# Score packs, value products and probability transfers regrouped over the two slots of a pair

## The chip, the cores and the metric

The kernel runs on one core of one Trainium2 chip. The metric is device time in microseconds (us) from start to end of one execution; lower is better. Engines in this document: PE (TensorE, matmul), PEld (its weight loads), DVE (VectorE), ACT (ScalarE), POOL (GpSimd), SP (SyncE, which here only issues transfers). Everything is float32.

## The reference, cut to what matters

Two layers run on x of shape (16, 256, 256). Layer 0 is a diagonal complex recurrence gated by a two-matrix MLP; the change leaves it alone. Layer 1 is causal attention with 16 heads over 256 positions, with compressed keys and values, gated by a mixture of LoRA experts:

```python
x = x + s * g                                   # layer 0
xn = _layernorm(x, axis=-1)
q = (x @ Wq).reshape(B, S, N_HEADS, QK_DIM)     # nope and rope parts
c_kv = c_kv * rsqrt(mean(c_kv * c_kv) + eps) * kv_norm_w
kv = (c_kv @ Wkv_b).reshape(B, S, N_HEADS, QK_NOPE + V_DIM)
scores = where(mask, einsum('bqhd,bkhd->bhqk', q, k) * scale, min)
attn = softmax(scores, axis=-1)
out = einsum('bhqk,bkhd->bqhd', attn, v).reshape(B, S, N_HEADS * V_DIM) @ Wo
g = silu(base(xn) + 2 * lora(xn))               # top 2 of 8 experts
x = x + out * g
```

The kernel folds the key and value expansions into the query and output weights, so keys and values have 64 latent columns (and 64 rope columns for the keys) that all heads share.

## The kernel before, in words

**Chunks, groups, units, slots.** The 4096 tokens are 8 chunks of 512 tokens, two batch rows each. Layer 0 runs chunk by chunk and fills about the first 266 us. Then a written-out loop (lines 1653 to 1745) runs over 64 units. Unit i belongs to chunk ch = i // 8; r = i % 8 is its place in the chunk. Its head group is n = i // 2 (four heads), its batch row is b = i % 2. One pass of the loop is called slot i here. Even slots have b = 0, odd slots b = 1; a pair of slots is one head group.

**The order is hand-written.** PE, DVE, ACT, POOL and SP are each wrapped in `InOrder` (lines 45 to 65), which chains every instruction to the one before it on that engine. So each engine runs its instructions in the order in which the loop writes them, and a wait holds up everything behind it on that engine. All these instructions are recorded with the wrapper's line, L53; the profile's groups are told apart by their tile names.

**One unit.** The 128 partitions hold 4 heads x 32 queries, and the 256 queries are 8 blocks a = 0..7; block a needs 32(a+1) keys.

- `score_pack(u, pi)`, lines 1369 to 1403: pack 0 is blocks 7 and 6, pack 1 is blocks 5, 4, 3, pack 2 (the short one) blocks 2, 1, 0. PE writes the pack's scores into one PSUM bank (tile `sc`, a pool of 3 banks); DVE adds the causal mask on the diagonals (`sc<-sc,kmask`) and takes negated row maxima (`nm<-sc`); ACT does the exponentials into `pr` with their sums in `sr` (`pr<-sc,nm`). Short packs of even units from i = 6 on are done as two halves of 64 weight columns (128*64 in the profile).
- `normalise(u, packs)`, line 1405: DVE takes reciprocals of `sr`, POOL multiplies `pr` by them (`pr<-pr,sr`).
- `turn(u, z)`, line 1418, z = 0, 1, 2: DVE transposes 32x32 blocks of `pr` into `turned`; z = 0 needs blocks 0 to 3, z = 1 and 2 need blocks 4 to 7.
- `send(u)`, line 1430: four DMAs from SP, 192 KB each, from `turned` to a DRAM tile `far`.
- `fetch(n, y, b)`, line 1444: one DMA from SP, 384 KB, reads half y of batch row b back into `pT`, of which there are 3 buffers. It waits until the sends of that row have landed.
- `values_of(n)`, line 1490: PE multiplies both rows of group n by the values, 16 products in float32 (32 records, four 64x64 tiles of the array at once), into two banks `av`; ACT copies them to `attT`.
- `turn_here`, line 1456: for the last two units PE transposes instead.

**Queries.** Group n is made ahead: `query_mm(n, t)` for t = 0..3 (two 512-column products each, tile `pq`), `query_mul` on DVE for t = 0, 1 (`qmul<-pq,rot_q`), `query_lat` on ACT for t = 2, 3 (`qg<-pq`), `query_rot` on POOL (`qrot`), and `query_move(n)`, eight 64 KB DMAs from SP.

**What else stands in the slots**, and the change leaves in its place: r = 0 `mid_chunk` (PE transposes `pmT`, ACT copies to `mT`), `gate_begin` (PE `pg`, whose third and sixth products read `mT`; DVE `h`, ACT tanh) and `norm_begin` (DVE statistics); r = 1 `gate_end` and `gate_begin`; r = 2 `gate_end`, `norm_end` (four DVE instructions `xn<-x,mv,rs`, behind pack 0's maxima), and at the slot's end `transpose_chunk` (PE `tp<-ident,xn`); r = 4 `kv_begin`; r = 5 `kv_end`; r = 6 `router_chunk` (PE `pm`, then some 20 small DVE instructions from `lg` to `mid`); r = 7 `key_chunk` (PE `pk`, ACT `kT`); and at r = 3, 4, 5, 7 `fast_end` (PE `po`, the output projection of the chunk before), with `fast_begin` on POOL at r = 4 to 7 and 0. PSUM tiles other than `sc` share 5 banks (pool `m1`).

**The slot before**, as PE runs it: even: pack 0, `pq` 3, pack 1, `values_of` for group (i-4)/2, pack 2, then what r adds; odd: pack 0, `pq` 0, pack 1, `pq` 1, pack 2, `pq` 2, then what r adds. Unit i's turns 1, 2, 0 and its send stand in slot i+1. Group n's fetches stand in slots 2n+2 (row 0) and 2n+3 (row 1), its products in slot 2n+4; `values_of(0)` is an exception and stands in slot 5.

Of the kernel before, what the change touches and what calls it, by code (L numbers as in the profile page):

```python
# [11 lines left out]
F32 = mybir.dt.float32  # L12
# [6 lines left out]
P = 128  # L19
B, S, D = 16, 256, 256  # L20
NTOK = B * S
CH = 512
# [19 lines left out]
def tile_two_layers(ctx: ExitStack, tc: tile.TileContext, d: dict, out: bass.AP):  # L42
# [384 lines left out]
        gp.tensor_tensor(q.rot[:, 0, :], m0[:, 0, :], m1_[:, 1, :], ALU.subtract)  # L427
        gp.tensor_tensor(q.rot[:, 1, :], m1_[:, 0, :], m0[:, 1, :], ALU.add)

    def query_move(n):  # L430
        q = groups[n]
        for r in range(2):
            for h in range(G):
                sp.dma_start(
                    q.qg[64 + 32 * r : 96 + 32 * r, :, h, :],
                    q.rot[32 * h : 32 * h + 32, r, :].rearrange("p (a q) -> p a q", q=32),
                )
# [921 lines left out]
    class Unit:  # L1359


        def __init__(self, i):
            self.i = i
            self.ch, r = divmod(i, 2 * NG)
            self.g, self.b = divmod(r, 2)
            self.n = f"{self.ch}_{self.g}_{self.b}"
            self.pr = prs[i % NPR]

    def score_pack(u, pi):
        k, b, pack = chunks[u.ch], u.b, PACK[pi]  # L1370
        if pi == 0:
            u.nm = sm1.tile([P, NQ], F32, tag="nm", name=f"nm_{u.n}", bufs=3)
            u.sr = sm1.tile([P, NQ], F32, tag="sr", name=f"sr_{u.n}", bufs=3)
        qg = groups[u.i // 2].qg
        sc = ps_sc.tile([P, CH], F32, tag="sc", name=f"sc_{u.n}_{pi}")
        halves = 2 if pi == 2 and u.b == 0 and u.i > 4 else 1
        m = P // halves
        for a, o in pack:
            w = qg[:, b * NQ + a, :, :].rearrange("p h q -> p (h q)")
            for y in range(halves):  # L1380
                pe.matmul(
                    sc[m * y : m * y + m, o : o + 32 * (a + 1)], w[:, m * y : m * y + m],
                    k.kT[:, b * S : b * S + 32 * (a + 1)], start=True, stop=True,
                )
        ends = [o + 32 * (a + 1) for a, o in pack]
        step = ends[1] - ends[0]
        n = len(pack)
        assert ends == [ends[0] + step * z for z in range(n)]
        if ends[0] - 32 + step * n <= CH:
            diag = sc[:, ends[0] - 32 : ends[0] - 32 + step * n].rearrange("p (n s) -> p n s", n=n)[:, :, 0:32]  # L1390
        else:
            diag = sc[:, ends[0] - step : ends[-1]].rearrange("p (n s) -> p n s", n=n)[:, :, step - 32 : step]
        ve.tensor_tensor(diag, diag, bc(kmask, n), ALU.add)
        for a, o in pack:
            ve.tensor_reduce(
                u.nm[:, a : a + 1], sc[:, o : o + 32 * (a + 1)], AX.X, ALU.max, negate=True
            )
        for a, o in pack:
            w = 32 * (a + 1)
            ac.activation(  # L1400
                u.pr[:, OFF[a] : OFF[a] + w], sc[:, o : o + w], AF.Exp,
                bias=u.nm[:, a : a + 1], accum_out=u.sr[:, a : a + 1],
            )

    def normalise(u, packs):
        blocks = [a for pi in packs for a, _ in PACK[pi]]
# [37 lines left out]
    def fetch(n, y, b):  # L1444

        q = groups[n]
        if y == b == 0:
            q.pT = {}
        if b == 0:
            q.pT[y] = pp.tile([P, G, 3 * P], F32, tag="pT", name=f"pT_{n}_{y}", bufs=3)  # L1450
        sp.dma_start(
            q.pT[y][64 * b : 64 * b + 64].rearrange("p h q -> p (h q)"),
            q.far[b].rearrange("(y k) s h z q -> y (k s) (h z q)", y=2)[y],
        )
# [198 lines left out]
    for i in range(LAST):  # L1653
        ch, r = divmod(i, PER)
        odd = i % 2 == 1
        u, w = units[i], units[i - 1] if i else None
        here = w is not None and w.i >= LAST - 2
        n = (i + 3) // 2 if odd else (i + 2) // 2
        n = n if n < len(groups) else None
        more = ch + 1 < NCH  # L1660
        last = ch - 1 if ch == NCH - 1 and r in FINISH else None
        fast = ch - 1 if 0 < ch < NCH - 1 else None

        if not odd and n is not None:
            query_move(n)
        if odd and i > 2:
            fetch((i - 3) // 2, 0, 1)
            fetch((i - 3) // 2, 1, 1)
        elif i and not odd:
            fetch((i - 2) // 2, 0, 0)  # L1670
        score_pack(u, 0)
        if w:
            normalise(w, (2,))
        if fast is not None and r > 3:
            fast_begin(fast, r)
        if ch > 1 and r == 0:
            fast_begin(ch - 2, 0)
        out_weights(i)
        if r == 1:
            gate_end(ch, 0)  # L1680
        if r == 2:
            gate_end(ch, 1)
            if more and ch:
                norm_end(ch + 1)
        if r == 5 and more:
            kv_end(ch + 1)
        if i == LAST - 1:

            finish_mm(last, 3, 0, NPAIR)
            finish_out(last, 3)  # L1690
            last = None
        if w:
            for z in (1, 2):
                turn_here(w, z) if here else turn(w, z)

        if r == 0:
            mid_chunk(ch)
        if r == 7 and more:
            key_chunk(ch + 1)
        if n is not None:  # L1700
            query_mm(n, 0 if odd else 3)
            if not odd:
                query_lat(n, 3)
        if i == 5:
            values_of(0)
        score_pack(u, 1)

        if odd and n is not None:
            query_mm(n, 1)
            query_mul(n, 0)  # L1710
        if w:
            if here:
                turn_here(w, 0)
            else:
                turn(w, 0)
                send(w)
        if not odd:
            if i > 4:
                values_of((i - 4) // 2)
            if i:  # L1720
                fetch((i - 2) // 2, 1, 0)
        score_pack(u, 2)
        normalise(u, (0, 1))

        if odd and n is not None:
            query_mm(n, 2)
            query_mul(n, 1)
            query_rot(n)
            query_lat(n, 2)
        if r < 2:  # L1730
            gate_begin(ch, r)
        if r == 0 and more and ch:
            norm_begin(ch + 1)
        if r == 2 and more:
            transpose_chunk(ch + 1)
        if r == 4 and more:
            kv_begin(ch + 1)
        if r == 6 and more:
            router_chunk(ch + 1)
        if last is not None:  # L1740
            j = FINISH.index(r)
            finish_mm(last, j, 0, NPAIR)
            finish_out(last, j)
        if fast is not None and r in FINISH:
            fast_end(fast, r)
# [1 line left out]

    ch = NCH - 1
    u0, u1 = units[LAST - 2], units[LAST - 1]
    normalise(u1, (2,))  # L1750

    finish_mm(ch, 0, 0, 4)
    finish_mm(ch, 1, 0, 4)
    values_of(LAST // 2 - 2)
# [85 lines left out]
```

## Time and profile before

| | us |
|---|---|
| median of 3 runs | 905.29 (903.8 to 905.55) |
| the profiled execution, its own time | 903.67 |
| its span, first to last instruction | 901.9 |
| PE busy / PEld busy | 889.3 / 666.8 |
| DVE busy | 667.4 |
| POOL busy | 571.2 |
| ACT busy | 476.0 |

The profile is of one execution. Its span is 1.8 us shorter than that execution's own time. "Busy" is the union of an engine's recorded instructions; PE's ends are modelled, so the start of the next record tells more than the end of one. Records of float32 products come in pairs (x2 in counts). In a timeline row, the columns are start, length, engine, line, operation, tiles, shape and count; a bracket gives idle time ahead of the row and what ended it. "PEclk" is the granted share of the TensorE clock. Matmul weights are given as 128*128, 128*64 or 64*64 (rows*columns of the array).

From DMA issue to landing the profile gives 4.4 us (median) for a `far<-turned` piece, 4.9 us for `pT<-far` and 2.7 us for `qg<-qrot`.

### The profile page before, as it was taken

To read this page: it belongs to the slowest core of one execution; us is meant where nothing else is said; L and a number is where in the kernel's file an instruction comes from. 1 tells how busy PE (TensorE), PEld (TensorE's weight loads), DVE (VectorE), ACT (ScalarE), POOL (GpSimd) and SP (SyncE) were. 2 spreads that over 40 slices of the span, in tenths; PEclk is the share of its full clock that TensorE was granted. 3 is DMA by queue.
4 is the path that set the end of the run, shared out by engine and by line. 5 is a ranking of instruction groups with operands and counts; after the bars stand their busy time and mean duration, and the time that the engine had idled before them with its cause. 6 is when DMAs were issued, how large, how long until landed. Compare 5 with 4: busy or idle time off the path is not lost.

```text
span 901.9 us, 17976 instructions
## 1 busy us (share of the span) xinstructions
PE 889.3 (99%) x5688; PEld 666.8 (74%) x5688; DVE 667.4 (74%) x2017; ACT 476.0 (53%) x1562; POOL 571.2 (63%) x885
## 2 busy tenths in 40 slices
PE   9999999999999989999999999999999999999988
PEld 8777999987757657776776777677677767766766
DVE  6886678764687869678868867886886788687642
ACT  3234665644436646655655565565556556556441
POOL 2229687787355537787586677758667775876531
PEclk9999999999999999999999999999999999999989
DMA  9730000000024888887887887788788768878880
GB/s 276 245 118 1 1 2 1 1 1 1 1 32 79 230 209 198 186 207 161 217 218 169 206 181 201 180 217 214 170 200 211 190 170 209 210 176 194 209 223 29
DMA packets 197406, 134.04 MB, mean 149 GB/s; under 512 B 143104, under 2 KB 187968, under 8 KB 197312
## 3 DMA queue, kind: packets, MB, share of 16 engines
q1 hardware_dynamic: 195184, 128.69, 58.0%
q0 software_dynamic: 1152, 3.67, 1.2%
q8 instruction: 46, 0.75, 0.4%
q10 hardware_dynamic: 976, 0.53, 0.2%
q14 instruction: 48, 0.39, 0.1%
HBM read 63.11 MB, written 52.95 MB: 129 GB/s over the span
## 4 chain that ended last, share of the span: by engine, by line
PE 93%; DVE 3%; DMA 2%; POOL 1%; ACT 1%; SPq 0%; issue 0%; ACTq 0%; POOLq 0%
PE pq L53 23%; PE sc L53 14%; PE po L53 11%; PE av L53 8%; PE f L53 7%; PE r L53 7%; PE pg L53 5%; PE ph L53 5%; PE pf L53 5%; PE pm L53 2%; PE pkv L53 2%; PE tp L53 2%; DMA far<-turned 1%; DMA pT<-far 1%; PE pb L53 1%; PE py L53 1%
## 5 line engine op out<-in xcount | busy, mean ns | idle before, releaser
L53 POOL TENSOR_SCALAR pr<-pr,sr 128x256 f32<-128x256 f32 (+7 forms) x512 | 192.5, 397 | 188.2 <-DVE sr L53 180.3
L53 ACT ACTIVATE pr<-sc,nm 128x256 f32<-128x256 f32 (+7 forms) x512 | 190.2, 382 | 217.1 <-DVE sr L53 139.6
L53 PEld LDWEIGHTS sc<-kT,qg 128*128 128x128 f32 (+1 forms) x1198 | 150.8, 176 | 54.8 <-issue 41.6
L53 PE MATMUL sc<-kT,qg 128*128 128x32 f32 (+6 forms) x1198 | 169.0, 290 | 0.0
L53 DVE TENSOR_REDUCE nm<-sc 128x1 f32<-128x256 f32 (+7 forms) x512 | 127.5, 301 | 6.6
L53 DVE STREAM_TRANSPOSE turned<-pr 128x512 f32<-128x512 f32 x186 | 123.2, 687 | 11.0 <-POOL pr L53 10.9
L53 PE MATMUL pq<-xnT,wlat 128*128 128x512 f32 x256 | 122.7, 602 | 0.0
L53 PE MATMUL pq<-xnT,wrope 128*128 128x512 f32 x256 | 120.2, 593 | 0.0
L53 ACT ACTIVATION_READ_ACCUMULATOR pr<-sc,nm 128x1 f32 x512 | 104.0, 203 | 0.0
L53 PE MATMUL av<-pT,rowv 64*64 64x512 f32 (+2 forms) x992 | 80.5, 445 | 6.0 <-DMA pT<-far 6.0
L53 POOL TENSOR_TENSOR qrot<-qmul,qmul 128x512 f32<-128x512 f32 x64 | 83.6, 1329 | 2.8 <-DVE qmul L53 2.8
L53 DVE TENSOR_TENSOR sc<-sc,kmask 128x96 f32<-128x96 f32 (+1 forms) x192 | 45.2, 236 | 53.8 <-PE sc L53 52.5
L53 DVE TENSOR_TENSOR qmul<-pq,rot_q 128x512 f32<-128x512 f32 x128 | 80.7, 672 | 0.1
L53 ACT ACTIVATE qg<-pq 64x512 f32<-64x512 f32 x128 | 75.5, 590 | 4.3 <-PE pq L53 3.5
L53 PEld LDWEIGHTS av<-pT,rowv 64*64 64x64 f32 x992 | 39.8, 135 | 43.6 <-issue 30.1
L53 PEld LDWEIGHTS pq<-xnT,wrope 128*128 128x128 f32 x256 | 45.7, 191 | 32.4 <-issue 32.1
L53 PEld LDWEIGHTS pq<-xnT,wlat 128*128 128x128 f32 x256 | 45.7, 191 | 31.6 <-issue 31.6
L53 PEld LDWEIGHTS po<-wout,attT 128*128 128x128 f32 x416 | 59.3, 193 | 9.8 <-issue 3.5
L53 PE MATMUL po<-wout,attT 128*128 128x128 f32 (+1 forms) x416 | 65.3, 311 | 0.0
L53 POOL TENSOR_TENSOR attT<-attT,attT 128x512 f32<-128x512 f32 x36 | 45.1, 1273 | 0.0
L53 POOL TENSOR_TENSOR rs<-ve,mhalf 128x4 f32<-128x4 f32 (+1 forms) x17 | 16.8, 987 | 41.1 <-DVE ve L53 33.6
L53 PE MATMUL pf<-p2T,hT 128*128 128x256 f32 x192 | 42.7, 380 | 0.0
(229 smaller groups left out, 1520.0 us busy)
## 6 DMA issues: line engine op xcount, KB each, us to landing
far<-turned SPq DMA_DIRECT2D x248, 192.0 KB, 4.4
pT<-far SPq DMA_DIRECT2D x124, 384.0 KB, 4.9
qg<-qrot SPq DMA_DIRECT2D x256, 64.0 KB, 2.7
x<-in_x_dram SPq DMA_DIRECT2D x7, 512.0 KB, 10.4
out_dram<-x POOLq DMA_DIRECT2D x12, 256.0 KB, 4.0
wqn_wo<-in_wq_nopeT_dram SPq DMA_DIRECT2D x4, 512.0 KB, 5.4
wqn_wo<-in_Wo_dram SPq DMA_DIRECT2D x4, 512.0 KB, 6.8
p2T<-in_proj2T_dram SPq DMA_DIRECT2D x2, 512.0 KB, 8.3
```

The source lines that it names most:

```text
L53: r = getattr(self.engine, name)(*args, **kw)
```

## The change

1. `score_pack` is split into `score_mm` (PE) and `score_exp` (mask, maxima, exponentials). Packs 0 and 1 go through the same steps as before.
2. The short packs of both units of a pair are done together, in the odd slot, by the new `score_small(w, u)`: both packs' products into one bank (the odd unit's at column 256), then `score_exp` of the even unit and `score_exp` of the odd unit. All short packs are now done in halves of 64 weight columns.
3. `values_of` moves from the even slots to the odd slots, directly ahead of `score_small`; group n's products stand in slot 2n+5 (group 0's already stood in slot 5).
4. The normalisations of blocks 2, 1, 0 of both units stand in the odd slot, behind `query_mul(n, 0)`.
5. Turn 0 and send of the even unit move to the next even slot, so that both sends of a pair stand there, with `query_move` between them (before, `query_move` stood first).
6. All four fetches of group n stand in slot 2n+3: row 0 and row 1 of half 0 at its start, half 1 behind `values_of`.
7. At the end, turn 0 of unit 62 (by PE) stands behind the last slot. `query_move` gets a parameter that no call uses.

```diff
@@ -1365,23 +1365,25 @@
             self.g, self.b = divmod(r, 2)
             self.n = f"{self.ch}_{self.g}_{self.b}"
             self.pr = prs[i % NPR]
-
-    def score_pack(u, pi):
-        k, b, pack = chunks[u.ch], u.b, PACK[pi]
-        if pi == 0:
+            self.nm = None
+
+    def score_mm(u, pi, sc, base=0):
+        k, b = chunks[u.ch], u.b
+        qg = groups[u.i // 2].qg
+        m = P // 2 if pi == 2 else P
+        for a, o in PACK[pi]:
+            w = qg[:, b * NQ + a, :, :].rearrange("p h q -> p (h q)")
+            for y in range(0, P, m):
+                pe.matmul(
+                    sc[y : y + m, base + o : base + o + 32 * (a + 1)], w[:, y : y + m],
+                    k.kT[:, b * S : b * S + 32 * (a + 1)], start=True, stop=True,
+                )
+
+    def score_exp(u, pi, sc, base=0):
+        if u.nm is None:
             u.nm = sm1.tile([P, NQ], F32, tag="nm", name=f"nm_{u.n}", bufs=3)
             u.sr = sm1.tile([P, NQ], F32, tag="sr", name=f"sr_{u.n}", bufs=3)
-        qg = groups[u.i // 2].qg
-        sc = ps_sc.tile([P, CH], F32, tag="sc", name=f"sc_{u.n}_{pi}")
-        halves = 2 if pi == 2 and u.b == 0 and u.i > 4 else 1
-        m = P // halves
-        for a, o in pack:
-            w = qg[:, b * NQ + a, :, :].rearrange("p h q -> p (h q)")
-            for y in range(halves):
-                pe.matmul(
-                    sc[m * y : m * y + m, o : o + 32 * (a + 1)], w[:, m * y : m * y + m],
-                    k.kT[:, b * S : b * S + 32 * (a + 1)], start=True, stop=True,
-                )
+        pack = [(a, base + o) for a, o in PACK[pi]]
         ends = [o + 32 * (a + 1) for a, o in pack]
         step = ends[1] - ends[0]
         n = len(pack)
@@ -1401,6 +1403,19 @@
                 u.pr[:, OFF[a] : OFF[a] + w], sc[:, o : o + w], AF.Exp,
                 bias=u.nm[:, a : a + 1], accum_out=u.sr[:, a : a + 1],
             )
+
+    def score_pack(u, pi):
+        sc = ps_sc.tile([P, CH], F32, tag="sc", name=f"sc_{u.n}_{pi}")
+        score_mm(u, pi, sc)
+        score_exp(u, pi, sc)
+
+    def score_small(u, v):
+
+        sc = ps_sc.tile([P, CH], F32, tag="sc", name=f"sc_{u.n}_2")
+        for z, y in enumerate((u, v)):
+            score_mm(y, 2, sc, z * S)
+        for z, y in enumerate((u, v)):
+            score_exp(y, 2, sc, z * S)
 
     def normalise(u, packs):
         blocks = [a for pi in packs for a, _ in PACK[pi]]
@@ -1661,16 +1676,10 @@
         last = ch - 1 if ch == NCH - 1 and r in FINISH else None
         fast = ch - 1 if 0 < ch < NCH - 1 else None
 
-        if not odd and n is not None:
-            query_move(n)
         if odd and i > 2:
+            fetch((i - 3) // 2, 0, 0)
             fetch((i - 3) // 2, 0, 1)
-            fetch((i - 3) // 2, 1, 1)
-        elif i and not odd:
-            fetch((i - 2) // 2, 0, 0)
         score_pack(u, 0)
-        if w:
-            normalise(w, (2,))
         if fast is not None and r > 3:
             fast_begin(fast, r)
         if ch > 1 and r == 0:
@@ -1689,6 +1698,11 @@
             finish_mm(last, 3, 0, NPAIR)
             finish_out(last, 3)
             last = None
+        if not odd and w:
+            turn(units[i - 2], 0)
+            send(units[i - 2])
+        if not odd and n is not None:
+            query_move(n)
         if w:
             for z in (1, 2):
                 turn_here(w, z) if here else turn(w, z)
@@ -1701,26 +1715,26 @@
             query_mm(n, 0 if odd else 3)
             if not odd:
                 query_lat(n, 3)
-        if i == 5:
-            values_of(0)
         score_pack(u, 1)
 
-        if odd and n is not None:
-            query_mm(n, 1)
-            query_mul(n, 0)
-        if w:
-            if here:
-                turn_here(w, 0)
-            else:
+        if odd:
+            if i > 4:
+                values_of((i - 5) // 2)
+            score_small(w, u)
+            normalise(u, (0, 1))
+            if i > 2:
+                fetch((i - 3) // 2, 1, 0)
+                fetch((i - 3) // 2, 1, 1)
+            if n is not None:
+                query_mm(n, 1)
+                query_mul(n, 0)
+            normalise(w, (2,))
+            normalise(u, (2,))
+        else:
+            if w:
                 turn(w, 0)
                 send(w)
-        if not odd:
-            if i > 4:
-                values_of((i - 4) // 2)
-            if i:
-                fetch((i - 2) // 2, 1, 0)
-        score_pack(u, 2)
-        normalise(u, (0, 1))
+            normalise(u, (0, 1))
 
         if odd and n is not None:
             query_mm(n, 2)
@@ -1747,8 +1761,8 @@
 
     ch = NCH - 1
     u0, u1 = units[LAST - 2], units[LAST - 1]
-    normalise(u1, (2,))
-
+
+    turn_here(u0, 0)
     finish_mm(ch, 0, 0, 4)
     finish_mm(ch, 1, 0, 4)
     values_of(LAST // 2 - 2)
```

In the order in which the changed kernel is built, PE runs in an even slot: pack 0, `pq` 3, pack 1, what r adds; in an odd slot: pack 0, `pq` 0, pack 1, values, both short packs, `pq` 1, `pq` 2, what r adds. The mask that DVE adds to the odd unit's short pack (`sc<-sc,kmask`, columns from 320) waits there for the last of ACT's three exponentials of the even unit's short pack, which read the same bank. The numbers of instructions on PE, DVE, ACT and SP that do the arithmetic and the transfers stay, but for 35 short packs that go from 3 products to 6 halves; POOL's stay too.

More of the change, by code (lines that the diff above doesn't have):

```diff
@@ L428, in query_rot, with query_move @@
         gp.tensor_tensor(q.rot[:, 1, :], m1_[:, 0, :], m0[:, 1, :], ALU.add)
-    def query_move(n):
+    def query_move(n, part=(0, 1)):
         q = groups[n]
-        for r in range(2):
+        for r in part:
             for h in range(G):
```

## The prediction

> **What bounds the kernel now.** First the page's busy times and its row of the granted clock.
>
> ```profile
> PE 889.3 (99%) x5688; PEld 666.8 (74%) x5688; DVE 667.4 (74%) x2017; ACT 476.0 (53%) x1562; POOL 571.2 (63%) x885
> PEclk9999999999999999999999999999999999999989
> ```
>
> PE sets the time: nothing shortens the span but less PE work, fewer PE gaps or a higher clock. Next PE's timeline, for gaps. After 270 us it has two of note, both waits for `pT`:
>
> ```profile
> 315.77 1.08 PE L53 MATMUL av<-pT,rowv 64*64 64x512 f32 x4
> 319.91 3.70 PE L53 MATMUL av<-pT,rowv 64*64 64x512 f32 x28 [3.07 <-DMA pT<-far]
> 323.54 0.59 PE L53 MATMUL sc<-kT,qg 128*64 128x96 f32 x12
> ...
> 859.95 1.07 PE L53 MATMUL av<-pT,rowv 64*64 64x512 f32 x4
> 863.81 1.51 PE L53 MATMUL av<-pT,rowv 64*64 64x512 f32 x16 [2.78 <-DMA pT<-far]
> ...
> 867.39 2.86 PE L53 MATMUL sc<-kT,qg 128*64 128x96 f32 x16
> 870.04 4.68 PE L53 MATMUL po<-wout,attT 128*128 128x256 f32 x16
> 874.55 1.04 PE L53 MATMUL pt<-ident,pr 128*128 128x128 f32 x8
> ```
>
> The rows behind a gap are long too. The stage table (stretch, PE busy, then the other engines; near the end the granted clock) tells why:
>
> ```profile
> 316.00:324.00 8.00, 4.93 (x44) 2.36 (x40) 2.93 (x9) 3.86 (x15) 3.41 (x6) 0.79 0.95 230
> 324.00:332.00 8.00, 8.00 (x50) 5.95 (x46) 6.08 (x30) 2.40 (x11) 2.07 (x5) 1.00 0.84 212
> ...
> 864.00:873.00 9.00, 8.83 (x53) 6.00 (x48) 1.88 (x9) 3.07 (x12) 2.94 (x8) 0.62 0.74 220
> ```
>
> A gap of about 3 us costs itself and then clock. Undisturbed values take 2.31 us, a halved short pack 0.52, pack 0 0.81, sixteen `po` 3.53 (854.70 to 858.23). So the first place lost 7.77 - 2.31 = **5.5 us**, the second 14.60 - 7.17 = **7.4 us**. Between them PE runs without gaps, at 78.2 us a chunk. Third, slot 34 (r = 2, from 510.95), PE and DVE:
>
> ```profile
> 514.39 2.46 PE L53 MATMUL av<-pT,rowv 64*64 64x512 f32 x32
> 516.78 0.59 PE L53 MATMUL sc<-kT,qg 128*64 128x96 f32 x12
> ```
>
> ```profile
> 511.96 0.23 DVE L53 TENSOR_TENSOR sc<-sc,kmask 128x64 f32<-128x64 f32 x1
> 512.23 0.72 DVE L53 TENSOR_REDUCE nm<-sc 128x1 f32<-128x256 f32 x2
> ...
> 512.95 0.88 DVE L53 SCALAR_TENSOR_TENSOR g<-g,h 128x512 f32<-128x512 f32 x1
> 513.76 2.36 DVE L53 TENSOR_SCALAR xn<-x,mv,rs 128x256 f32<-128x256 f32 x4
> ```
>
> `xn` ends at 516.12; `tp` reads it at 517.30, 1.2 us later. Values and short pack are the cover.
>
> **Step 1: the `pT` gaps go, -12.9 us.** Group n's fetches stand in slot 2n+3, its products in 2n+5; between lie some 19 us of PE work. From the last send (median 4.4 us to landing) through a fetch (4.9) is 9.3 plus issues of about 0.6 each. The first gap came from a fetch that had to wait for `values_of(0)` to free a buffer; that too is now a pair earlier. If this cover is not enough, each gap costs what it cost above.
>
> **Step 2: fewer PE microseconds, -4 us.** A full short pack takes 0.59 (505.97 to 506.56), a halved one 0.52, of which about 0.19 is its start and end: its own records come 0.03 to 0.08 apart, 0.33 in all. Two in a row: 0.85, against 1.11 now, so 0.26 for each of 32 pairs, 8 us. About half of the pairs lose it again to the waits below.
>
> **Step 3: even slots get too short.** They lose 2.31 + 0.52 of PE work, and DVE's, ACT's and POOL's parts stay. Prices by start-to-start times of the rows near 552 to 571 us: DVE mask and maxima of pack 0 0.90, pack 1 0.98, a short pack 0.67; one transpose 0.63, two 1.20; `qmul` 1.19; reciprocal 0.13; ACT exponentials of pack 0 0.90, pack 1 1.13, short 0.87; both `attT` copies 0.98, `mT` or `kT` 0.55.
>
> *Step 3a, r = 2.* `tp` is now reached 0.81 + 1.72 + 0.81 = 3.34 us into the slot. Even with DVE on time, `xn` is ready at 5.1 (as above, less a reciprocal); the first three of the eight transposes are done by then, five at 0.11 to 0.12 are left, so the floor is 1.35 us (5.65 for the 4.3 of an undisturbed slot), in the six chunks that have `norm_end`.
>
> *Step 3b, a new wait on DVE.* The odd unit's mask waits for ACT's last exponential of the even unit's short pack. Behind it on DVE stand the maxima, `qmul` and reciprocals; POOL's normalisation waits for those. Where DVE is on time this is 1 us and hidden. Where DVE is late, ACT has pack 1 (1.13), both `attT` copies (0.98) and the short pack (0.87) to do first, while DVE does 0.67: 2.3 us more (1.13 + 0.98 + 0.87 - 0.67) of DVE's chain, which is then the longer one.
>
> *Step 3c, r = 6 to 2 by this.* Times from the start of slot r = 6, DVE on time (first free at 1.02, after `fast_end`): 0.90 + 0.63 + 1.20 + 0.98 to 4.73, exponentials to 6.0, router from the second `lg` on 5.26 (560.45 to 565.71 now), to 11.7. PE ends the slot at 5.3 and is at r = 7's `po` at 16.0. DVE: 0.90 + 1.20 + 0.98, to 14.8; ACT: 1.13, first `attT` copy, 16.6. `po` takes that `av`'s bank: **0.65** late. Short pack, second mask (18.1), `qmul` to 20.1: `pq` 3 in slot r = 0, which takes that bank, is **0.4** late. DVE goes on with reciprocals, `qmul`, `c`, pack 0 to 22.8, ACT's exponentials and `mT` to 24.4; `pg`'s third product is there at 23.55: **0.9** late. Now `mT` is in time because values and short pack stand ahead of `pg`. DVE then has 0.63 + 1.20 + 0.98, ACT 1.13, `h` and statistics 2.45, to 29.55; slot r = 1: 0.90 + 0.7 + 1.20 + 0.98 + 0.67, wait to 36.5, 0.67 + 0.13 + 1.19 + 0.2 + 1.2, to 40.0; then `h` 0.65, pack 0 0.90, `g` 0.7, `xn` to 44.6. PE is at `tp` at 42.4 and leaves it at 45.25 for 43.3: **1.9** late. From there DVE catches up by r = 5. A chunk loses 3.9 us: 6 x 3.9, and 1.2 for the first change of chunk (no `po` there): **+24.6 us**. Floor 8 (step 3a alone); with DVE's row lengths for start-to-start times, which overlap by some 6%, the same walk gives 6 to 7 a chunk: 42.
>
> **Step 4: the end, +10 us.** After slot 61 few queries are left to fill PE. In slot 63 `pt` of unit 62 waits for its POOL normalisation, which needs pack 1's exponentials: 1.8 us. Then turn 0 of unit 62 stands right behind the last short packs with no PE work between. From their end at 0: mask, maxima and exponentials of the even unit, mask and maxima of the odd one to 2.6, reciprocal, POOL's five products of unit 63 (2.03, as at 510.02) and three of unit 62 (0.90): PE idles **5.7 us**. By the two gaps above the clock then halves, 3.4 to 6.8 us long: 1.7 to 3.4, I take 2.5. Between 5.7 and 12.
>
> **The clock.** A gap of 1.05 us (at 72.21, behind `wlat`) shows no loss of clock, those of 2.78 and 3.07 do. Step 3a's gap of 1.9 is between: 0 to 1.7 us in each of six chunks. I take a third, **+3.5 us**. [...]
>
> **Sum**: 901.9 - 12.9 - 4 + 24.6 + 10 + 3.5 = 923.1, and 1.8 around the span as now: **925 us**. The profiled execution (903.67) is 1.6 below the median of the runs.
>
> **Moved for nothing.** `query_move` stands behind a send that waits for turn 0: some 5 us later than now, for scores a pair away. Transfers are the same in number and size; three turns a slot become four and two, the sum is unchanged. If that cover went, `qg` would hold pack 0 by what is missing.
>
> **The rivals.**
> - *DVE and ACT keep pace* (**faster**). Steps 1 and 2 in full, 20.9; against them step 3a's floor 8 and step 4 without clock 5.7: 894.7, so **897**. For it: DVE is busy only 74%. Against: steps 3b and 3c's order. It decides when all new waits stay under 20.9.
> - *Only the floors and the end with its clock*: 901.9 - 16.9 + 8 + 10, so **905**.
> - *DVE's chain sets the pace* in all pairs, or the clock falls in every chunk: 42 and 10 for 24.6 and 3.5, **949**.
> - *The transfers don't get their lead*, since both sends now collide with `query_move` in the even slot: both gaps stay, **938**. DMA is at 80 to 90% already; against it, step 1's 19 us for 9.3 plus issues.
>
> **Numbers.** Forecast 925 (from 908 to 945): 62%. DVE keeps pace: 15%. Floors only: 10%. DVE sets the pace: 10%. No lead: 3%. About 0.2%, 1.8 us, is what a measurement of this kernel tells from no change. Floors-only is split evenly between no change and slower: faster 0.15, same 0.05, slower 0.80. The range 901 to 945 takes in the floors and leaves out most of the first rival and the third.
>
> **What would show it.** No DMA wait of `av`; `tp` idle for DVE `xn` in six chunks, for 1.3 to 3 us; `sc<-sc,kmask` on DVE waiting for ACT `pr` 32 times, 1 to 2.5 us each; `po`, `pq` and `pg` waiting for `attT`, `qmul`, `mT` around r = 7 and 0; `pt` near the end idle above 5 us for POOL `pr`; the clock halved behind it. The forecast is wrong if `tp` follows `sc` without a gap, or if PE's work between gaps, with clock, takes over 78 us a chunk.

## The result, and the profile after

The changed kernel takes **984.15 us** (median of 5 runs, 980.85 to 986.33) against 904.26 for the kernel before on the same chip (903.61 to 905.55): ratio **1.088**, 95% interval 1.085 to 1.090. The forecast was 925, its range 901 to 945. The direction was right, the size was not: 80 us instead of 20.

The page of the changed kernel, whose profiled execution took 986.33 us (span 984.6): busy times, granted clock, and the chain of work that ended last.

```profile
PE 911.8 (93%) x5898; PEld 667.9 (68%) x5898; DVE 732.9 (74%) x2017; ACT 475.0 (48%) x1562; POOL 563.9 (57%) x885
PEclk9999999999999999999998998999899899999979
PE 53%; DVE 25%; ACT 7%; POOL 5%; issue 4%; DMA 3%; SPq 2%; DVEq 0%; POOLq 0%; ACTq 0%
```

In the kernel before, the same chain was

```profile
PE 93%; DVE 3%; DMA 2%; POOL 1%; ACT 1%; SPq 0%; issue 0%; ACTq 0%; POOLq 0%
```

PE is idle for 72.8 us of the span (12.6 before) and busy 22.5 us longer although it has less to do: from 270 us on to 15 us before the end it ran at half clock for 68.3 us, against 10.2. DVE's share of time is 74% in both kernels, but of a longer time: with the same 2017 instructions it is busy 732.9 us against 667.4. The chain says more: a quarter of it is now DVE.

PE's timeline at r = 7 and r = 2 of one chunk of the changed kernel:

```profile
508.90 1.98 PE L53 MATMUL pq<-xnT,wrope 128*128 128x512 f32 x4
516.10 3.78 PE L53 MATMUL pq<-xnT,wlat 128*128 128x512 f32 x4 [5.21 <-ACT kT L53]
...
544.30 0.98 PE L53 MATMUL sc<-kT,qg 128*128 128x192 f32 x6
546.84 1.74 PE L53 MATMUL tp<-ident,xn 128*128 128x128 f32 x8 [1.56 <-DVE xn L53]
```

The second product group behind the 5.2 us gap takes 3.78 us where the undisturbed one takes 1.88; from 516 to 520 us the granted clock was 0.50. The waits of `av` for `pT` are gone, as step 1 said. PE's largest waits are for `kT` (33.0 us in 7 places), `xn` (11.0 in 6) and, at the end, `pr` (9.8 in 2).

DVE's waits between 350 and 850 us, first before, then after (total, times, longest):

```profile
DVE sc L53 <- PE sc L53: 38.1, 40, 2.9
DVE keep L53 <- PE po L53: 14.5, 6, 2.4
```

```profile
DVE sc L53 <- ACT pr L53: 49.8, 22, 2.5
DVE sr L53 <- ACT pr L53: 16.4, 22, 0.7
DVE sc L53 <- PE sc L53: 13.8, 17, 2.2
```

An engine that keeps up waits for the one that sets the pace. Before, DVE waited for PE's scores; after, it waits for ACT, and for PE's scores only in 17 places. Its waits for PE of all kinds in this window fell from 78.7 to 14.3 us. This is a sign, not yet a proof. The first line of the second list (`sc` for ACT `pr`) is step 3b's new wait. In the whole run it is 70.7 us in 32 places.

A chunk, from one chunk's first `pkv` row to the next (mean of the five behind chunk 2), takes 78.6 us before and **89.6** after. This period is the yardstick below.

### The profile page after: what moved, and what is told of

Same layout as the page of the kernel before. It is cut to its first block, busy times and chain, and to the rows that moved or that the text cites. A ratio compares the mean times of both kernels' runs of the same rounds, so it can differ in the third digit from the quotient of the medians.

```text
span 984.6 us, 18321 instructions
## 1 busy us (share of the span) xinstructions
PE 911.8 (93%) x5898; PEld 667.9 (68%) x5898; DVE 732.9 (74%) x2017; ACT 475.0 (48%) x1562; POOL 563.9 (57%) x885
## 4 chain that ended last, share of the span: by engine, by line
PE 53%; DVE 25%; ACT 7%; POOL 5%; issue 4%; DMA 3%; SPq 2%; DVEq 0%; POOLq 0%; ACTq 0%
PE pq L53 10%; PE f L53 6%; PE r L53 6%; ACT pr L53 5%; PE sc L53 5%; DVE nm L53 5%; DVE turned L53 4%; PE ph L53 4%; PE pf L53 4%; PE po L53 4%; DVE qmul L53 3%; PE pg L53 3%; PE av L53 3%; DVE g L53 2%; POOL pr L53 2%
## 5 line engine op out<-in xcount | busy, mean ns | idle before, releaser
L53 POOL TENSOR_SCALAR pr<-pr,sr 128x128 f32<-128x128 f32 (+7 forms) x512 | 187.7, 391 | 276.9 <-DVE sr L53 275.1
L53 ACT ACTIVATE pr<-sc,nm 128x128 f32<-128x128 f32 (+7 forms) x512 | 190.2, 384 | 248.6 <-DVE nm L53 213.2
L53 PEld LDWEIGHTS sc<-kT,qg 128*64 128x64 f32 (+1 forms) x1408 | 139.1, 164 | 46.8 <-issue 26.8
L53 PE MATMUL sc<-kT,qg 128*64 128x64 f32 (+7 forms) x1408 | 161.3, 279 | 4.1 <-DVE sc L53 2.4
L53 PE MATMUL pq<-xnT,wlat 128*128 128x512 f32 x256 | 132.2, 643 | 33.0 <-ACT kT L53 33.0
L53 DVE TENSOR_REDUCE nm<-sc 128x1 f32<-128x128 f32 (+7 forms) x512 | 127.5, 301 | 6.6
L53 DVE STREAM_TRANSPOSE turned<-pr 128x512 f32<-128x512 f32 x186 | 120.4, 684 | 11.9 <-POOL pr L53 8.3
L53 PE MATMUL pq<-xnT,wrope 128*128 128x512 f32 x256 | 126.1, 617 | 0.0
L53 DVE TENSOR_TENSOR sc<-sc,kmask 128x64 f32<-128x64 f32 (+1 forms) x192 | 46.0, 240 | 93.5 <-ACT pr L53 70.7
L53 PEld LDWEIGHTS pq<-xnT,wlat 128*128 128x128 f32 x256 | 50.8, 204 | 85.3 <-issue 44.8
L53 PE MATMUL ph<-xnT,p1T 128*128 128x256 f32 (+1 forms) x128 | 42.6, 487 | 0.0
```

Source lines behind the costliest of these rows:

```text
L53: r = getattr(self.engine, name)(*args, **kw)
```

## The experiments

Each ratio is against the kernel before, run beside it on the same chip.

| label | made from | median us | ratio (95%) | period us |
|---|---|---|---|---|
| key_first | after | 985.61 | 1.087 (1.084 to 1.090) | 90.1 |
| pool_late | after | 988.38 | 1.090 (1.087 to 1.093) | 90.2 |
| turn_later | after | 988.20 | 1.088 (1.085 to 1.092) | 90.1 |
| masks_first | after | 920.81 | 1.015 (1.013 to 1.018) | 80.7 |
| maxima_twice | after | 994.25 | 1.096 (1.093 to 1.098) | 90.9 |
| maxima_twice_before | before | 909.36 | 1.004 (1.002 to 1.006) | 79.2 |
| values_even | after | 1010.91 | 1.115 (1.112 to 1.118) | 92.7 |
| short_single | after | 931.67 | 1.027 (1.025 to 1.030) | 81.9 |
| pool_out | after | 965.12 | 1.064 (1.062 to 1.067) | 86.2 |
| pool_in_router | before | 922.66 | 1.017 (1.014 to 1.020) | 80.9 |
| masks_router_end | masks_first | 909.08 | 1.003 (1.002 to 1.005) | 78.9 |
| cover_gaps | before | 906.52 | 1.001 (0.999 to 1.003) | 79.1 |
| mended | masks_router_end | 906.24 | 1.002 (1.000 to 1.004) | 78.6 |
| mended_single | mended | 913.57 | 1.011 (1.009 to 1.013) | 79.9 |
| mended_turn | mended | 910.56 | 1.009 (1.006 to 1.012) | 79.8 |

### First theory: the router, held up by POOL

The gap at `pq` 2 is the largest, and what ends it is `kT`. ACT copies `kT` behind pack 0's exponentials, which wait for DVE, which does the router first. In the kernel before, the router takes 4.92 us from `ex` to `mid`; here it takes 9.6. DVE's rows at r = 6 of the changed kernel, then POOL's:

```profile
503.99 3.15 DVE L53 TENSOR_TENSOR ex<-lg,m 128x32 f32<-128x32 f32 x1
...
508.09 1.31 DVE L53 TENSOR_TENSOR oh<-desc,fm 128x32 f32<-128x32 f32 x1
```

```profile
503.93 1.43 POOL L53 TENSOR_TENSOR c<-v,keep 128x256 f32<-128x256 f32 x2
505.30 0.74 POOL L53 TENSOR_TENSOR keep<-keep 128x256 f32<-128x256 f32 x1
506.00 2.12 POOL L53 TENSOR_SCALAR pr<-pr,sr 128x256 f32<-128x256 f32 x5
508.09 1.26 POOL L53 TENSOR_TENSOR c<-c,g 128x512 f32<-128x512 f32 x1
```

`ex` and `oh` each take 0.19 us where POOL runs nothing (from 247.03 us), here 3.15 and 1.31; `oh` ends at 509.40, POOL's `c` beside it at 509.35. Theory A made this the cause.

The router is not the only place; the theories below don't reckon with the others. It accounts for some 28 us of the 65.5 that DVE is busy longer. Two other groups of the changed kernel, over the whole run (total in us, mean in ns):

```profile
L53 DVE SCALAR_TENSOR_TENSOR g<-g,h 128x512 f32<-128x512 f32 x16 | 28.8, 1800 | 0.0
L53 DVE TENSOR_TENSOR row<-tmp,kvw_bc 128x256 f32<-128x256 f32 x8 | 22.8, 2846 | 0.3
```

In the kernel before they take 11.9 and 3.6 us in all, and `ss`, a scaling of four columns in `kv_begin`, takes 1.4 us there and 11.0 here. In one chunk of the changed kernel `g` lasts 2.77 us from 543.69 (r = 2), `ss` 2.79 from 569.86 (r = 4) and `row` 3.64 from 575.06 (r = 5), all three while POOL runs `qrot` or `attT`.

Four kernels each took away one thing.

**key_first** moves two lines:

```diff
+        if r == 7 and more:
+            key_chunk(ch + 1)
         score_pack(u, 0)
...
-        if r == 7 and more:
-            key_chunk(ch + 1)
```

> The changed kernel with key_chunk ahead of pack 0 in slot r = 7, so that ACT copies kT before the exponentials that wait for DVE, and the bank that pq 2 takes comes free without the router. Theory A (DVE's router chain is 9.6 us instead of 4.9 because its instructions with two SBUF inputs stand still while POOL's run, and all of DVE is late behind it): the gap at pq 2 goes, but the output projection of r = 7 then waits for the first attT copy, which stands behind the same late exponentials; by a walk from 513.5 us in the trace (maxima 0.9, transposes 1.2, maxima 1.0, exponentials 1.1, copy 0.5) it starts 1.4 us earlier per chunk than now at the most: 974 to 984. Rival B (only this bank and the place of the copy are at fault): all of 5.2 us and its clock is gained in seven chunks, about 36 and as much again for the clock, some 913.

985.61. The gap at `pq` is gone and stands one step on, in PE's list of waits:

```profile
PE po L53 <- ACT attT L53: 42.2, 11, 6.3
PE tp L53 <- DVE xn L53: 10.2, 6, 2.6
```

Rival B falls: the bank and the copy are only where the lateness is felt.

**pool_late** computes `c1` in place, in `p4` and `p5`, at the end of slot 7, where `fast_begin(fast, 8)` is called:

```diff
         elif r == 6:
             fast_sum(ch, (1, 0), (1, 0), (0, 0), ALU.subtract)
-            k.c1 = a2.tile([P, 2, D], F32, tag="h", name=f"c1_{ch}", bufs=1)
-            gp.tensor_tensor(k.c1[:, :, 0:DH], k.v, k.p4, ALU.subtract)
-            gp.tensor_tensor(k.c1[:, :, DH:D], k.v, k.p5, ALU.add)
             gp.tensor_tensor(k.u, k.u, k.p5, ALU.add)
-        elif r == 7:
-            fast_out(ch, 1, k.c1, (0, 1))
+        elif r == 8:
+            gp.tensor_tensor(k.p4, k.v, k.p4, ALU.subtract)
+            gp.tensor_tensor(k.p5, k.v, k.p5, ALU.add)
+            fast_out(ch, 1, k.p4, (0,))
+            fast_out(ch, 1, k.p5, (1,))
             fast_store(ch, 1)
```

> The changed kernel with POOL's subtraction, addition, multiplication and addition of the second half of the output (fast_begin 6 and 7 but for the attT sums and one addition to keep) moved from the router's time to the end of slot 7, with the same results. Theory A: the router chain, from ex to mid, falls from 9.6 to about 5.6 us, the gap at pq 2 from 5.2 to about 1.2, too short to lower the clock by what gaps of 1 us showed: 4 us and about 2.6 of clock in six chunks, 944 (930 to 955). Rival B (bank) and rival C (the short even slots alone make DVE late): the chain stays near 9.6 or PE does not follow it, 978 to 986.

988.38. The router fell to 5.6 us (6.4 in two chunks) and the gap at `pq` to 1 to 2 us, as theory A wanted, and nothing was gained. Its PE now waits for `attT` at `pg` (16.6 us), and its DVE for POOL's `pr` 15.7 us between 350 and 850 (4.7 in the changed kernel): the moved work came back at the next turn. By the table below, r = 6 and 7 take 5.0 us less than in the changed kernel, and r = 0 and 1 take 4.9 more. Theory A's number is refuted; whether its mechanism counts stayed open.

**turn_later**: `if r == 2 and more: transpose_chunk(ch + 1)` becomes `r == 3`.

> The changed kernel with transpose_chunk at the end of slot r = 3 instead of r = 2, so that tp no longer stands 3.3 us behind the slot's start. The wait of tp for xn (11.0 us in six chunks) goes. Theory A: it is a second and smaller loss, 11 us and 0 to 10 of clock: 965 to 975. Rival C (the short even slot is what costs most): over 25 us, below 960.

988.20. `tp` no longer waits for `xn`, but 9.3 us for `attT`, and `po` 13.9 us for `qmul`. Again the wait moved: r = 2 and 3 take 4.3 us more than in the changed kernel, and r = 6 and 7, which DVE then reaches on time, 2.7 less.

**masks_first** splits `score_exp` and does both units' masks and maxima first:

```diff
         for z, y in enumerate((u, v)):
+            score_max(y, 2, sc, z * S)
+        for z, y in enumerate((u, v)):
             score_exp(y, 2, sc, z * S)
```

> The changed kernel with masks and maxima of both short packs ahead of the six exponentials, so that DVE's wait for ACT in the odd slot (70.7 us in 32 places) goes. Theory A: in most slots this wait lies beside PE work; what is gained is at r = 7 to 1, where DVE is late, up to 2.3 us in a few places: 970 to 984. Rival D (this wait is what makes DVE late everywhere): the other gaps shrink with it by 2 us or more each, below 955.

**920.81**: by the ratios 66 us of the 80 are gone, far more than theory A allowed. Rival D holds. DVE in slot r = 3, first of the changed kernel, then of masks_first:

```profile
556.11 0.26 DVE L53 TENSOR_TENSOR sc<-sc,kmask 128x96 f32<-128x96 f32 x1
556.40 0.49 DVE L53 TENSOR_REDUCE nm<-sc 128x1 f32<-128x96 f32 x3
559.36 0.27 DVE L53 TENSOR_TENSOR sc<-sc,kmask 128x96 f32<-128x96 f32 x1 [2.47 <-ACT pr L53]
559.66 0.49 DVE L53 TENSOR_REDUCE nm<-sc 128x1 f32<-128x96 f32 x3
```

```profile
528.34 0.26 DVE L53 TENSOR_TENSOR sc<-sc,kmask 128x96 f32<-128x96 f32 x1
528.63 0.49 DVE L53 TENSOR_REDUCE nm<-sc 128x1 f32<-128x96 f32 x3
529.15 0.27 DVE L53 TENSOR_TENSOR sc<-sc,kmask 128x96 f32<-128x96 f32 x1
...
535.45 0.23 DVE L53 TENSOR_TENSOR sc<-sc,kmask 128x64 f32<-128x64 f32 x1 [1.62 <-PE sc L53]
```

The two masks follow each other without the 2.47 us, and at the next slot DVE waits 1.62 us for PE. In the changed kernel it waits 0.5 to 2.2 us at that place, so this alone tells little. **Theory E**, formed here: DVE's chain, with its waits for ACT, sets the pace over a large part of each chunk.

Where the time goes shows better by pairs of slots (PE, from pack 0 of one pair to pack 0 of the next, us, mean of chunks 2 to 6):

| kernel | r = 0, 1 | r = 2, 3 | r = 4, 5 | r = 6, 7 |
|---|---|---|---|---|
| before | 19.4 | 18.5 | 22.8 | 17.9 |
| after | 19.2 | 21.5 | 23.3 | 25.3 |
| pool_late | 24.1 | 22.9 | 22.6 | 20.3 |
| turn_later | 19.3 | 25.8 | 22.5 | 22.6 |
| masks_first | 19.2 | 18.3 | 22.5 | 20.6 |
| maxima_twice | 19.3 | 22.7 | 22.8 | 26.0 |
| pool_out | 19.7 | 22.1 | 23.0 | 21.2 |

The changed kernel loses 7.4 us a chunk at r = 6 and 7 and 3.0 at r = 2 and 3; the other four slots lose 0.3 together. DVE is hardly late there: its router (second `lg`) starts 6.98 us into slot r = 6, against 6.31 in masks_first. POOL is late: its normalisation and `qrot` wait for the reciprocals and `qmul` that stand behind the wait on DVE. Its block of r = 6, up to `keep`, ends 9.45 us into the slot, inside the router; in masks_first it ends at 6.26, ahead of it, and the router takes 6.6 to 7.0 us instead of 9.6. At r = 2 `g` starts at 1.92 us in both kernels; POOL's `qrot` runs there from 1.69 to 4.20 in the changed kernel and is over at 2.06 in masks_first, and `g` takes 2.8 and 0.7 us (medians of six chunks). So the order of the masks costs 66 us, which is shown; that most of it goes by way of POOL's work beside DVE's is read from these times. For r = 6, pool_out and pool_in_router bear on it below; for r = 2 no run tests it alone.

### Testing theory E

**maxima_twice** and its control add the two `tensor_reduce` instructions of pack 0 a second time where `u.b == 1`.

> The changed kernel with pack 0's two maxima of odd units done twice (same results), which adds 0.64 us of DVE work (start to start) to each of 32 odd slots, well ahead of the wait for ACT. Theory E, formed from masks_first: DVE's chain with its wait for ACT (70.7 us in 32 places) sets the pace of the changed kernel, and the gaps on PE only show where it is felt. Then all of it is paid: 32 x 0.64, 20 us, 1004 (1000 to 1008). Theory A (the router's hold-up is the loss, the rest of DVE has slack): only what falls into slots r = 7 and 1 is paid, a quarter to a half, 989 to 994.

> The same addition made to the kernel before, as the control. Both theories: PE sets the pace there and DVE has slack, so nearly nothing of 20 us is paid: within 4 us of the kernel before.

Against the changed kernel, 10 us of 20 are paid by the medians, 7 by the ratios; the period grows by 1.3, two of its four additions. In the kernel before it is 0.4% (0.2 to 0.6), about 3 us. So 1004 was wrong, and of the two numbers theory A's is nearer: by the table, the addition is paid at r = 2 and 3 (1.2 us) and r = 6 and 7 (0.7), not in the other slots. The chain of the changed kernel between 503 and 594 us runs on DVE, ACT and POOL in r = 6 and 7, on PE from 516 to 543 (r = 7 to 2), then on DVE, ACT and POOL with hardly any PE up to the next r = 7; PE keeps level with them at r = 4 and 5, where it loses 0.5 us. Theory E, and its narrower form E2 in the expectations below (from r = 6 to r = 2), say too much: DVE has little time in hand in most slots, but time is lost in four of eight.

**values_even**:

```diff
-            if i > 4:
-                values_of((i - 5) // 2)
+            if i == 5:
+                values_of(0)
             score_small(w, u)
...
                 send(w)
+            if i > 4:
+                values_of((i - 4) // 2)
             normalise(u, (0, 1))
```

> The changed kernel with values_of back in the even slots (group n in slot 2n+4), the rest of the change kept. ACT then no longer has the two attT copies (0.98 us) between pack 1's exponentials and the even unit's short ones, so DVE's wait in the odd slot falls from 2.5 to about 1.5 us. Theory E: 32 x 0.98, 31 us less, about 953; as the fetches stand as late as now, a wait of av for pT may take some of it back: 945 to 970. Theory A or C: it is a matter of cover at r = 2 alone, 11 us and its clock: 965 to 975.

1010.91, slower still. DVE's wait fell to 1.50 us as reckoned (33.0 us in 22 places between 350 and 850), but `av` now waits for `pT` in 19 places (13.9 us), DVE waits up to 10.1 us once a chunk for ACT's `tmp` (40.1 us in 5 places), and 95.6 us run at half clock (mean granted clock 0.953). At 570 us the two hang together: PE reaches `pkv`, which `tmp` reads, late behind such an `av`. With all fetches in the odd slot, products in the next even slot come too early. The two moves belong together; theory E had allowed this wait 17 us at most.

**short_single**:

```diff
-            score_small(w, u)
+            score_pack(u, 2)
             normalise(u, (0, 1))
...
                 send(w)
+            score_pack(u, 2)
             normalise(u, (0, 1))
```

> The changed kernel with the short packs single again, each at the end of its own unit's slot ahead of the normalisation of packs 0 and 1 (halves for even units as before); values, sends and fetches stay where the change put them. Theory E: the second mask's wait is gone, as in masks_first, and the even slots get 0.52 us of PE work back: 915 (905 to 925). Theory A: the even slots are still short of the values' 2.3 us and POOL's work still falls on the router, 960 to 980.

931.67: 6.7 above theory E's range, far from theory A's. Most of DVE's long instructions are gone here too (`row` 3.6 us in all, `ss` 1.4; DVE busy 676.2). It splits the change: by the ratios, later products and transfers cost 25 us (2.7%), the paired short packs, as written, 55 more.

### Is the hold-up by POOL a cost of its own?

**pool_out** leaves out what pool_late moved: in `fast_begin`, the two `k.c1` instructions of r = 6 and the `fast_out` of r = 7.

> The changed kernel without POOL's subtraction, addition, multiplication and addition of the second half of the output (left out: the second half of a chunk's rows in six chunks get no layer 1); the attT sums and one addition to keep stay. In pool_late this work was only moved, and POOL then came late with the next unit's probabilities. Theory E2 (DVE's chain sets the pace from r = 6 to r = 2, and the router's hold-up is a part of it): the router falls to 5.6 us, 4 us less in each of six chunks, and the clock with it: 945 to 965. Rival F (what is saved there is taken back by other waits, as in the three kernels that moved a single thing): 978 to 988.

965.12, period 86.2: 3.4 us a chunk, at the edge of theory E2's range. The router fell to 6.4 us, not 5.6; r = 6 and 7 take 4.1 us less than in the changed kernel. So the hold-up in the router is a real part, once the work isn't given back elsewhere. `g`, `ss` and `row` still take 29.8, 9.5 and 22.8 us: their hold-up was not tested by itself.

**pool_in_router** makes it in the kernel before: `fast_begin(fast, 6)` is called behind `normalise(u, (0, 1))` instead of behind pack 0.

> The kernel before with POOL's block of r = 6 (attT sums 2.5 us, c 1.4, keep 0.7) behind the slot's normalisation instead of ahead of it, so that it runs beside the router's instructions on DVE. If POOL's two-input instructions hold up DVE's, the router grows from 4.9 to about 9 us with nothing of the change present; if the router is long in the changed kernel for another reason, it stays at 4.9. The time: PE sets the pace and DVE has slack, so 0 to 2 us per chunk, 905 to 920.

The router grows from 4.9 to 7.24 us in each chunk, with nothing of the change present. DVE's two longest instructions of it, and POOL beside them:

```profile
488.33 0.99 DVE L53 TENSOR_TENSOR oh<-desc,fm 128x32 f32<-128x32 f32 x1
489.35 1.19 DVE L53 SCALAR_TENSOR_TENSOR l<-oh,lg 128x32 f32<-128x32 f32 x1
```

```profile
488.00 2.49 POOL L53 TENSOR_TENSOR attT<-attT,attT 128x512 f32<-128x512 f32 x2
```

It was to be 9. And the time grew by 1.7%, some 15 us, 2.3 us a chunk: at r = 6 and 7 the kernel before has little slack on DVE, or on POOL, whose block now ends later; the run doesn't tell the two apart.

### Putting it right

**masks_router_end**: masks_first, and the router's chain (now `router_end`) in slot 7 behind pack 1's maxima, and the last pair's short packs as before:

```diff
         score_pack(u, 1)
+        if r == 7 and more:
+            router_end(ch + 1)
```

**cover_gaps**: the kernel before, with `values_of(1)` behind slot 6's router products, and in slot 62 `finish_mm(last, 3)` and pack 2 ahead of `values_of(29)`.

> masks_first and two more: the router's chain on DVE stands behind pack 1's maxima of slot r = 7 instead of at the end of slot r = 6 (its products stay), and the last pair does its short packs singly, as before, so that turn 0 of unit 62 needs not wait at the end. Theory E2: PE sets the pace throughout; of masks_first's span of 919.0 the waits for kT (11.6), attT (2.7) and at pt (8.2) go, with 2 of clock: 894.5, time 896 (890 to 902). If other waits take their place (qmul's bank, late short packs): 905 to 920.

> The kernel before with its two waits of av for pT covered by moving PE's work alone: values_of(1) behind the router's products of slot 6, values_of(29) behind the short pack and the last output projection of chunk 6 in slot 62. Of the 12.9 us that the prediction's step 1 counted there, about 10 should go without any of the change: 895 (892 to 900). Rival: attT copies then come late for the output projection, or the work put ahead was itself cover in slot 63: 902 to 908.

masks_router_end: 909.08, period 78.9, router 4.8. Of the 11.0 us a chunk 10.7 are gone: 8.9 with the masks, 1.8 with the router. But it is not the 896 expected, and not below the kernel before: PE now waits 7.8 us for `mT`, 3.4 for `pr` and 2.4 for `attT`. cover_gaps: no difference, the rival's answer. Its `av` waits at 338.0 us for 1.97 and at 882.3 for 3.54: work put in front of one group hands the wait to the next. That the transfers are late there as a stream is a reading of this, not shown.

**mended** goes on from masks_router_end: `mid_chunk` ahead of pack 0 at r = 0, the first router back in slot 6, `values_of(29)` ahead of pack 1 in slot 63. **mended_single** has single short packs on top (short_single's edit).

> masks_router_end with its three remaining losses mended: mid_chunk ahead of pack 0 in slot r = 0 (ACT copies mT before pack 0's exponentials, on which pg waits 0.6 to 1.1 us in six chunks), the router's chain left in slot 6 in the first change of chunk (there no POOL work of a chunk before runs; it lost 5.3 us against masks_first), and values_of(29) ahead of pack 1 in slot 63 (po waits 2.1 us for attT). Theory E2 (PE sets the pace once no DVE wait stands in its way, and then steps 1 and 2 are kept): 909 - 5 - 5 - 2, 897 (893 to 901), below the kernel before. If not: 903 to 910, and the regrouping is worth nothing even without its waits.

> mended with the short packs single, each at the end of its own slot, which leaves the later products and transfers as the only part of the change. Step 2 of the prediction says that pairing them saves 0.26 us in each of 32 pairs: 4 to 8 us more than mended, 901 to 905. If a single short pack in the even slot is useful cover for DVE, it is the same or faster.

mended: 906.24, 1.002 (1.000 to 1.004); not the 897 expected. mended_single: 913.57, so the pairing is worth 7 us (8 by the ratios). What still costs in mended is seen at r = 2, in PE's timeline:

```profile
517.65 0.98 PE L53 MATMUL sc<-kT,qg 128*128 128x192 f32 x6
519.04 1.74 PE L53 MATMUL tp<-ident,xn 128*128 128x128 f32 x8 [0.41 <-DVE xn L53]
520.61 0.97 PE L53 MATMUL sc<-kT,qg 128*128 128x256 f32 x4
```

From 517.65 to 520.61 are 2.96 us for 1.75 undisturbed (0.82 and 0.93); the loss is 1.2 us in four of the six chunks, 1.5 and 2.7 in the others. `g`, which stands ahead of `xn` on DVE, takes 1.62 us there beside POOL's `qrot`. In masks_router_end it takes 0.75, and the same stretch 2.09 us. Moving `mid_chunk` gained 1.5 us a chunk at r = 0 and 1; 0.9 of it went at r = 2 and 3, 0.5 at r = 6 and 7.

**mended_turn** takes `tp` to the end of slot 3, behind `fast_end`.

> mended with transpose_chunk at the end of slot r = 3, behind the output projection, instead of at the end of slot r = 2. In mended's records pack 1 and tp of r = 2 take 3.07 us (1.50 + 1.57) where 0.82 + 0.93 is what they take undisturbed: 1.32 us lost in each of six chunks, the floor of 1.35 that the prediction's step 3a gave. Theory E2: this is the last thing between the regrouping and its gain: 906.2 - 6 x 1.32 = 898 (896 to 901), below the kernel before. In the changed kernel itself the same move gained nothing (turn_later), since DVE was late there anyway. Rival: tp waits for a bank or for attT at its new place, 904 to 908.

910.56, by the ratios 6 us slower than mended: the rival's wait came, and its 904 to 908 was still too low. `po` at r = 3 now waits for `attT`, 10.5 us in 6 places. No version beat the kernel before, and whether one exists is open.

## Why the prediction was wrong, by its steps

- **Step 1** was right in mechanism: the two gaps are gone, and products two slots behind their fetches are what the late fetches need (values_even). That the 12.9 us are gained in full was not shown: in mended `av` waits 1.4 us for `pT` in all, and it still isn't faster; in cover_gaps the gaps only moved.
- **Step 2** was right: the two packs take 0.92 us from first row to next group (0.85 forecast), 0.19 less than the two single ones; the pairing is worth 7 to 8 us (8 in full, 4 after the waits forecast), once its wait is gone.
- **Step 3a** had the wait of `tp` for `xn` right and its size wrong: 1.35 is no floor. It counts 2.36 us for `xn`, a length that these four rows had beside POOL's `qrot` (512.02 to 514.97); in the changed kernel, with POOL idle, they take 1.37. In masks_router_end the stretch loses 0.3 us in five of six chunks. That mended loses 1.2 is luck for the number: there it is `g` that POOL holds up. In the changed kernel the loss is 2.3 to 3.3 us.
- **Step 3b** had the wait's size, 2.3 us, measured 2.47 at r = 3. It failed in "Where DVE is on time this is 1 us and hidden": at r = 1, where DVE had just waited 0.31 us for PE, it is 2.07. Hidden from PE it is: r = 4 and 5 lose 0.5 us. It isn't hidden from POOL, whose normalisation the same step names as waiting: POOL is 3.2 us later at r = 6 and 2.1 at r = 2 than in masks_first.
- **Step 3c** is the step that failed, in its price of the router: 5.26 us, "to 11.7" in the slot. The router takes 9.9 by the same rows and ends at 17.0; `kT` follows, and r = 6 and 7 lose 7.4 us, clock included, where the walk had `po` 0.65 late. The price came from a trace in which POOL's block of r = 6 had just ended; the walk gave POOL beside DVE no term, though step 3b's wait is what makes POOL late. At r = 2 the same was missing from `g` (0.7, measured 2.8), and r = 2 and 3 lose 3.0 for the walk's 1.9. "A chunk loses 3.9 us" became 11.0. What the walk assumed of DVE held nearly: it enters r = 6 at 1.70 us instead of 1.02, and "From there DVE catches up by r = 5" is 0.7 us off. The walk missed that `pq` 2 takes `pk`'s bank; key_first shows that this cost nothing by itself.
- **Step 4** was of the right size: `pt` waits of 3.8 and 6.0 us for 1.8 and 5.7 forecast. From the last `pkv` to PE's end, masks_first takes 135.4 us and masks_router_end 128.6, 6.8 less, of which some 1.8, the difference of their periods, are the router's place: so 5 for 10.
- **The clock** was far off: 6 us forecast with steps 3 and 4; 58 us more at half clock than before cost some 26 us (PE is busy 911.8 against 885.5 in masks_first, the same instructions).
- **The rivals.** "DVE's chain sets the pace" came nearest with 949, at 10%, but not by its mechanism: time is lost in two of the four pairs of slots, not in all. "DVE and ACT keep pace", argued from DVE's 74%, was refuted by a DVE that was again busy 74%, of a time 82.7 us longer.
- **Readings.** The 78.2 us a chunk of the kernel before are 78.6 by its `pkv` rows, so the last sign of being wrong (over 78 us a chunk) would have been met by the kernel before. Some times of the walk lie up to 0.4 us above their own terms (22.8 + 0.63 + 1.20 + 0.98 + 1.13 + 2.45 is 29.2, not 29.55). Neither changes the outcome.

## What to carry to other kernels

Where an in-order engine gets a new wait, follow it to every engine that waits for this one, and see beside what their work comes to lie: here DVE was 0.7 us late, POOL 3.2, and that brought POOL's block onto the router. A price taken from a trace holds only beside the neighbours that it had there. When taking away one gap leaves the time unchanged and a new gap appears, compare the time stretch by stretch to see where it went. Do all that frees the next engine (here both masks) before the instruction that waits for it.

## What the runs showed of the hardware

**The clock.** In the trace of the changed kernel the half-clock stretches behind layer 0 are 3.41 or 6.83 us long, and they start whole multiples of 3.413 us apart (300.18 to 955.54 us). With the time from 285 to 895 us divided at that spacing, in this trace and in that of the kernel before, PE's idle time was counted in each division. Of the divisions at full clock, the eleven with 1.91 us or more idle were all followed by one at half clock, of the eight with 1.36 to 1.90 three, of those with 1.35 or less none. The second halves of the 6.83-us stretches don't fit this count: the divisions ahead of them have 0.13 (before, 865.35 us) to 2.87 us idle. In the changed kernel the gap of 1.68 us at `tp` (to 725.26 us) was followed by half clock from 726.85 us on, the gap of 1.70 at `pq` (to 334.48 us) by none. PE's ends are modelled, which blurs these numbers.

**DVE and POOL.** In six chunks of the changed kernel `ex`, `eq<-l,m` and `oh<-desc,fm`, instructions of DVE with two inputs from SBUF, took 3.13 to 3.15, 0.92 to 0.93 and 1.31 us beside TENSOR_TENSOR instructions of POOL; at 327 to 329 us, where POOL ran only `pr<-pr,sr`, 0.23, 0.19 and 0.19. `ss`, with one input, took up to 2.79 for 0.17. It is not so beside each such instruction: `l<-oh,lg` took 0.19 us beside POOL's `x<-x,c` (509.43 us). One `ex`, from 503.99 to 507.14 us, lasted through three TENSOR_TENSOR instructions of POOL on end (503.93 to 506.04 us) and into its `pr`. Why DVE's are long there is not shown.

**What stands ahead** goes with small differences in PE's lengths, from 330 us on and where no gap and no half clock disturbs: in the changed kernel `pq` by `wrope` took 1.82 us, to the next group's start, behind the halved short packs (20 times) and 1.72 behind pack 0 (16); in the kernel before `pq` by `wlat` took 1.80 behind a single short pack (27) and 1.72 behind pack 0 (20).
